# A first stage with VectorE in the program's order, inputs one step ahead, outputs and routing one step later, and joint norms by Newton

## The chip, the cores and the metric

The kernel runs on one core of a Trainium2 chip. The metric is the device time of one execution in microseconds (us), the median of three runs. Engines are named as in the profile: PE is TensorE's matrix products and PEld its weight loads, DVE is VectorE, ACT is ScalarE, POOL is GpSimd, SP is SyncE, which issues most of the DMAs. L404 is line 404 of the kernel before.

## The reference, cut to what matters

Two layers act on x of 8 batches, 512 tokens, 256 channels, in float32. Each layer is an attention and a mixture of experts, both behind a layer norm that is scaled and shifted per batch, and both added back through a gate per batch.

```python
mod = (silu(c) @ wmod).reshape(8, 6, 1, 256)        # sa, ca, ga, sb, cb, gb
h = layernorm(x) * (1 + ca) + sa
x = x + ga * attention(h)
h = layernorm(x) * (1 + cb) + sb
x = x + gb * experts(h)

# layer 0, attention: 16 heads of 64 channels
q = tanh(h @ W_Q) * pi / 4; k = tanh(h @ W_K) * pi / 4      # one number per token and head
heads = cos(q) * cumsum(cos(k) * V) + sin(q) * cumsum(sin(k) * V)
heads /= cos(q) * cumsum(cos(k)) + sin(q) * cumsum(sin(k)) + 1e-6
out = einsum('deh,bthe->btd', W_O, heads)

# layer 0, experts: the best 2 of 4 by softmax; silu(x w1) * (x w3) @ w2
# layer 1, attention: softmax attention in 4 groups of 16 heads, gated
# layer 1, experts: the best 1 of 8 by sigmoid; gelu(x W1) @ W2
```

## The kernel before, in words

The tokens of a batch are four tiles (t) of 128 tokens on the partitions; x of all batches stays in SBUF. A scheduler puts the instructions of each engine into an order. Apart from dependences, that order is its own choice; the program's order (the order in which the Python issues the instructions) is a starting point only. Within an engine's queue, instructions then run in the order chosen.

*The first stage.* Layer 0's attention goes by batch, 0 to 3 (`first`), then most of batch 4, before the first line of experts starts.

- `prepare0(b)` (L329): the norm of b (`norm_T`, with its statistics in `stats`, L175), transposes, the small products `pq`, tanh, then cos and sin by ACT into `tr`, the running sums `pd` by products with a triangle of ones, the denominators `rd` on DVE (L362 to L369), and three sets of rows by token, copied by ACT (L376) and written to DRAM by POOL (L381, L382, `rows`).
- `heads0(b, j)` (L385), eight steps j of two heads each: SP loads `ratio` and `factor`, spread over 64 partitions each, from `rows` (L391); PE makes the values `pv` (L398); DVE runs two scans (L404), which are the two running sums, a multiplication (L407) and an addition (L409) into `hd`.
- `out0(b, t)` (L412): eight products `poa` of `hd` with W_O (L415), then `residual` (L223): DVE multiplies by the gate into `tmp`, of which there are two buffers (L226), and POOL adds it to x (L227).
- `attend0(b)` (L420) runs the eight steps with `prepare0(b + 1)` let in at j = 0, 3 and 5, and then the four `out0`.
- `Moe.route(i)` (L475) for the batch before: norm statistics `stf` of x, the normed rows into `ht`, the slot numbers into `ht` and `ht1` by POOL (L491; `ht1` has one buffer), transposes, the router's product `pl` (L504), softmax and the two best experts by some 24 small DVE instructions (L520 to L558), the ranks `pk` (L563), the positions `pos` (L575) and eight scatters by POOL (L579), which put each token's row at its expert's place in DRAM (`hs`). `table` (L592) makes from the counts the list of expert tiles.
- Beside it: `load_rest`, which holds layer 1's modulation (L136 to L166), and `order_wq`, which reorders a weight.

The loop is `drain(weave(attend0(b), chain(m0.route(b - 1), wq_steps)))`: one step of the side work after each step of the main work. Then route of batch 3, `table`, and seven steps of `a1`, which is `attend0(4)` and what follows.

*The rest.* `Line.run` goes through the list of expert tiles: `xs` loaded by SP (L720), transposed, products `p` (L753), Silu and a multiplication (L758, L760), products `po` (L768), a scaling and a scatter of results. It takes steps of side work (`a1`; later layer 1's attention) between the tiles. Layer 1's attention (`attend`) handles four batches jointly, in two halves; `norm_T` makes their norms. In `stats` ACT takes the square root, DVE the reciprocal, and one Newton step follows:

```python
        nc.scalar.activation(r, v, AF.Sqrt)
        nc.vector.reciprocal(r, r)
        n = wk.tile([P, NT], F32, tag="newton", name=f"newton{nm}")
        nc.vector.scalar_tensor_tensor(n, r, -0.5, r, ALU.mult, ALU.mult)
        nc.vector.tensor_mul(n, n, v)
        nc.vector.scalar_tensor_tensor(r, n, 1.5, r, ALU.add, ALU.mult)
```

Of the kernel before, what the change touches and what calls it, by code (L numbers as in the profile page):

```python
# [9 lines left out]
F32 = mybir.dt.float32  # L10
# [18 lines left out]
def kernel(  # L29
# [99 lines left out]


# [3 lines left out]
    def modulation(l, c, wmod, mp):  # L134
# [4 lines left out]
        for n in range(3):  # L139
# [3 lines left out]
            for kk in range(KD):  # L143
                nc.tensor.matmul(pr[:B, :], sc[:, kk, :], wm[:, kk, :], start=(kk == 0), stop=(kk == KD - 1))
            rows = mp.tile([B, 2, D], F32, tag="rows", name=f"rows{l}_{n}", bufs=1)
            nc.vector.tensor_copy(rows.rearrange("b c d -> b (c d)"), pr[:B, :])
            for i in range(2):
                j = 2 * n + i
                if j % 3 == 1:
                    nc.vector.tensor_scalar(rows[:, i], rows[:, i], 1.0, None, ALU.add)  # L150
                elif j % 3 == 2:
                    sgn = mp.tile([B, D], F32, tag="sgn", name=f"sgn{l}_{j}", bufs=1)
                    nc.vector.tensor_scalar(sgn, rows[:, i], 0.0, 2.0, ALU.is_ge, ALU.mult)
                    mag = mp.tile([B, D], F32, tag="mag", name=f"mag{l}_{j}", bufs=1)
                    nc.scalar.activation(mag, rows[:, i], AF.Abs)
                    nc.vector.tensor_scalar(mag, mag, GATE_MIN, None, ALU.max)
                    nc.vector.scalar_tensor_tensor(rows[:, i], sgn, -1.0, mag, ALU.add, ALU.mult)
            by_channel = [i for i in range(2) if (2 * n + i) % 3 != 2]
            pm = ps_m([P, len(by_channel), KD, B], f"pmT{l}_{n}")
            for m, i in enumerate(by_channel):  # L160
                for k in range(KD):
                    nc.tensor.transpose(pm[:, m, k, :], rows[:, i, k * P : (k + 1) * P], ident[:B, :B])
            at = (0, 2, 3)[n]
            nc.vector.tensor_copy(modT[l][:, at : at + len(by_channel)], pm)
# [10 lines left out]
    def stats(b, nm):  # L175
# [3 lines left out]
        for t in range(NT):  # L179
            nc.vector.bn_stats(st[:, t, :], x[b][:, t, :])  # L180
            nc.vector.bn_aggr(mv[:, t, :], st[:, t, :])
        v = wk.tile([P, NT], F32, tag="var", name=f"var{nm}")
        nc.vector.tensor_scalar(v, mv[:, :, 1], LN_EPS, None, ALU.add)
        r = wk.tile([P, NT], F32, tag="rstd", name=f"rstd{nm}")
        nc.scalar.activation(r, v, AF.Sqrt)
        nc.vector.reciprocal(r, r)
        n = wk.tile([P, NT], F32, tag="newton", name=f"newton{nm}")
        nc.vector.scalar_tensor_tensor(n, r, -0.5, r, ALU.mult, ALU.mult)
        nc.vector.tensor_mul(n, n, v)
        nc.vector.scalar_tensor_tensor(r, n, 1.5, r, ALU.add, ALU.mult)  # L190
        return mv, r

    def normed(b, mv, r, dst, nm):

        sh = wk.tile([P, NT], F32, tag="sh", name=f"sh{nm}")
        nc.vector.scalar_tensor_tensor(sh, mv[:, :, 0], -1.0, r, ALU.mult, ALU.mult)
# [11 lines left out]
    def norm_T(l, b, dst):  # L208


        mv, r = stats(b, f"{l}_{b}")
        xn = wk.tile([P, NT, D], F32, tag="xn", name=f"xn{l}_{b}", bufs=1)
        normed(b, mv, r, xn, f"{l}_{b}")
        for k in range(KD):
            pt = ps_m([P, NT, P], f"pt{l}_{b}_{k}")
            for t in range(NT):
                nc.tensor.transpose(pt[:, t, :], xn[:, t, k * P : (k + 1) * P], ident)
# [5 lines left out]
    def residual(po, gate, b, t, name):  # L223

        tmp = wk.tile([P, D], F32, tag="tmp", name=name, bufs=2)
        nc.vector.tensor_mul(tmp, po, gate)  # L226
        nc.gpsimd.tensor_tensor(x[b][:, t, :], x[b][:, t, :], tmp, ALU.add)  # L227
# [101 lines left out]
    def prepare0(b):  # L329
# [4 lines left out]
        for t in range(NT):  # L334
            for k in range(KD):
                nc.tensor.matmul(
# [21 lines left out]
        nc.tensor.matmul(pd, tri, c, start=True, stop=False)  # L358
        nc.tensor.matmul(pd[:, 1:], ones, before, start=False, stop=True)
        ab = tr[:, :, 2]  # L360
        rd = ap.tile([P, NT, H], F32, tag="rd", name=f"rd{b}", bufs=1)
        nc.vector.tensor_mul(ab, sq, pd)  # L362
        nc.vector.tensor_add(rd, ab[:, :, 0, :], ab[:, :, 1, :])
        nc.vector.tensor_scalar(rd, rd, DEN_EPS * math.sin(2 * ALPHA), None, ALU.add)
        nc.vector.reciprocal(rd, rd)
        nc.vector.reciprocal(tr[:, :, 1], c)
        for i in range(2):
            nc.vector.tensor_mul(ab[:, :, i], sq[:, :, i], rd)
        nc.vector.tensor_mul(ab, ab, c)  # L369
        pt = ps_m([3 * 2 * H, NT, P], f"ptr{b}")  # L370
        for t in range(NT):
            nc.tensor.transpose(pt[:, t, :], tr[:, t].rearrange("p a i h -> p (a i h)"), ident)
# [6 lines left out]
        nc.vector.tensor_mul(rows[1][:, 1:], rows[1][:, 1:], rows[0][:, : S - 1])  # L379
# [5 lines left out]
    def heads0(b, j):  # L385
# [11 lines left out]
        for k in range(KD):  # L397
            nc.tensor.matmul(  # L398
                pv, wv_sb[:, k, j * P : (j + 1) * P], hTs[b][:, k, :],
                start=(k == 0), stop=(k == KD - 1),  # L400
            )
        u = ap.tile([P, 2, S], F32, tag="u", name=f"u{b}_{j}", bufs=2)
        for i in range(2):
            nc.vector.tensor_tensor_scan(  # L404
                out=u[:, i], data0=w[0][:, i], data1=pv, initial=0.0, op0=ALU.mult, op1=ALU.add
            )
        nc.vector.tensor_mul(u, u, w[1])  # L407
        hd = ap.tile([P, S], F32, tag="hd", name=f"hd{b}_{j}", bufs=9)
        nc.vector.tensor_add(hd, u[:, 0], u[:, 1])  # L409
        return hd  # L410

    def out0(b, t, hds, ga):  # L412
        po = ps_o(f"poa{b}_{t}")
        for j in range(NJ):
            nc.tensor.matmul(  # L415
                po, hds[j][:, t * P : (t + 1) * P], wo_sb[:, j, :], start=(j == 0), stop=(j == NJ - 1),
            )
        residual(po, ga, b, t, f"ra{b}_{t}")

    def attend0(b):  # L420

# [3 lines left out]
        for j in range(NJ):  # L425
            hds.append(heads0(b, j))
            if j in (0, 3, 5):
                next(nxt, None)
            yield
        for t in range(NT):  # L430
            out0(b, t, hds, ga)
        yield

    hTs = {}
# [10 lines left out]
    def first_max(v, E, m, o, name):  # L445


        nc.vector.tensor_reduce(m, v, AX.X, ALU.max)
        nc.vector.tensor_tensor(o, v, bcast(m, E), ALU.is_equal)
        nc.vector.tensor_mul(o, o, desc[:, :E].unsqueeze(1).to_broadcast([P, NT, E]))  # L450
        k = wk.tile([P, NT], F32, tag="rm", name=f"k{name}", bufs=4)
        nc.vector.tensor_reduce(k, o, AX.X, ALU.max)
        nc.vector.tensor_tensor(o, o, bcast(k, E), ALU.is_equal)

    class Moe:
# [19 lines left out]
        def route(self, i):  # L475
# [9 lines left out]
            h0 = ht[0]  # L485
            mv, r = stats(b, f"f{bm}")
# [9 lines left out]
            for k in range(KD):  # L496
                pt = ps_m([P, NT, P], f"ptr{bm}_{k}")
                for t in range(NT):
                    nc.tensor.transpose(pt[:, t, :], h0[:, t, k * P : (k + 1) * P], ident)
                by_channel(l, 2, k, b, hT[:, k], pt.rearrange("p t q -> p (t q)"))  # L500
            pl = ps_m([P, NT, E], f"pl{bm}")
            for t in range(NT):
                for k in range(KD):
                    nc.tensor.matmul(  # L504
# [3 lines left out]
            for t in range(0, NT, 2):  # L508
                pb = ps_m([P, 2, D], f"prow{bm}_{t}")
                for q in range(2):  # L510
                    for k in range(KD):
                        nc.tensor.transpose(
# [7 lines left out]
            nc.vector.tensor_tensor(z, pl, b_sb.unsqueeze(1).to_broadcast([P, NT, E]), ALU.add)  # L520
# [6 lines left out]
            if l == 0:  # L527
                s = wk.tile([P, NT], F32, tag="rs", name=f"s{b}")
                nc.vector.tensor_reduce(s, z, AX.X, ALU.max)
                nc.vector.tensor_tensor(z, z, bcast(s, E), ALU.subtract)  # L530
                nc.scalar.activation(z, z, AF.Exp)
                nc.vector.tensor_reduce(s, z, AX.X, ALU.add)
                nc.vector.reciprocal(s, s)
                nc.vector.tensor_mul(z, z, bcast(s, E))
                first_max(z, E, m[0], ch[0], f"a{b}")
                nc.vector.scalar_tensor_tensor(z, ch[0], -2.0, z, ALU.mult, ALU.add)
                first_max(z, E, m[1], ch[1], f"b{b}")
                now = wk.tile([P, NT, E], F32, tag="now", name=f"now{bm}", bufs=2)
                nc.vector.tensor_add(now, ch[0], ch[1])
                nc.vector.tensor_add(s, m[0], m[1])  # L540
                nc.vector.reciprocal(s, s)
                for c in range(C):
                    nc.vector.tensor_mul(ht[c][:, :, D + 1], m[c], s)
            else:
                nc.scalar.activation(z, z, AF.Exp, scale=-1.0)
                nc.vector.tensor_scalar(z, z, 1.0, None, ALU.add)
                nc.vector.reciprocal(z, z)
                first_max(z, E, m[0], ch[0], f"c{b}")
                now = ch[0]
                nc.vector.tensor_copy(ht[0][:, :, D + 1], m[0])  # L550

            pre = fp.tile([P, NT + 1, E], F32, tag=f"pre{E}", name=f"pre{bm}", bufs=3)
            if i == 0:
                nc.vector.memset(pre[:, 0], 0.0)
            else:
                nc.vector.tensor_copy(pre[:, 0], self.run_)
            for t in range(NT):
                nc.vector.tensor_add(pre[:, t + 1], pre[:, t], now[:, t])  # L558
# [3 lines left out]
            nc.tensor.matmul(pk, tri, now, start=True, stop=False)  # L562
            nc.tensor.matmul(pk, ones, pre[:, :NT], start=False, stop=True)  # L563
            yield
            rank = wk.tile([P, NT, E], F32, tag="rank", name=f"rank{bm}", bufs=2)
            nc.vector.tensor_tensor(
# [4 lines left out]
            for c in range(C):  # L571
                nc.vector.tensor_mul(at, ch[c], rank)  # L572
                p_ = fp.tile([P, NT], I32, tag=f"pos{c}", name=f"pos{c}_{bm}", bufs=3)
                with nc.allow_low_precision("whole numbers"):
                    nc.vector.tensor_reduce(p_, at, AX.X, ALU.add)  # L575
# [16 lines left out]
        def table(self):  # L592
# [3 lines left out]
            nc.tensor.matmul(pn, ones, self.run_, start=True, stop=True)  # L596
            n = wk.tile([P, E], F32, tag="cnt", name=f"cnt{nm}", bufs=1)
            nc.vector.tensor_copy(n, pn)
            past_ = fp.tile([1, E1], I32, tag="pasts", name=f"past{nm}", bufs=2)[:, :E]
            nc.vector.scalar_tensor_tensor(past_, n[0:1], 1.0, cbase[0:1, :E], ALU.add, ALU.add)  # L600
            self.past = past_
            cmp_ = wk.tile([P, E, TH], F32, tag="cmp", name=f"cmp{nm}", bufs=1)
            nc.vector.tensor_tensor(
# [3 lines left out]
            nc.vector.tensor_reduce(nt, cmp_, AX.X, ALU.add)  # L607
            upto = wk.tile([P, E, E], F32, tag="upto", name=f"upto{nm}", bufs=1)
            nc.vector.tensor_tensor(
# [3 lines left out]
            nc.vector.tensor_reduce(end, upto, AX.X, ALU.add)  # L613
            base = wk.tile([P, E], F32, tag="base", name=f"base{nm}")
            nc.vector.tensor_sub(base, end, nt)
            full = [P, J, E]

            def of_tile(v, op, rows, dst, name, weigh=None):

                t_ = wk.tile(full, F32, tag="past", name=f"{name}{nm}", bufs=1)  # L620
                nc.vector.tensor_tensor(
                    t_, bcast(rows[:, :J], E), v.unsqueeze(1).to_broadcast(full), op
                )
                if weigh is not None:
                    nc.vector.tensor_tensor(t_, t_, weigh.unsqueeze(1).to_broadcast(full), ALU.mult)
                nc.vector.tensor_reduce(dst, t_, AX.X, ALU.add)
# [4 lines left out]
            nc.vector.tensor_scalar(self.tab[:, 0], which, float(E - 1), None, ALU.min)  # L631
            nc.vector.tensor_scalar(nt, nt, -1.0, float(CAP), ALU.mult, ALU.add)
            skip = wk.tile([P, J], F32, tag="skip", name=f"skip{nm}", bufs=1)
            of_tile(end, ALU.is_ge, iota, skip, "rows", weigh=nt)
            nc.vector.tensor_add(skip, skip, iota[:, :J])
            nc.vector.tensor_scalar(self.tab[:, 1], skip, float(P), float(E * CAP * P), ALU.mult, ALU.min)

            lim = wk.tile([P, E], F32, tag="lim", name=f"lim{nm}", bufs=1)
            nc.vector.scalar_tensor_tensor(lim, base, float(P), n, ALU.mult, ALU.add)
# [3 lines left out]
            nc.vector.tensor_sub(self.used, self.used, skip)  # L643
            self.rest = fp.tile([P, JMAX], F32, tag="rest", name=f"rest{nm}", bufs=2)[:, :J]
            nc.vector.scalar_tensor_tensor(
# [5 lines left out]
        def keep(self, end):  # L651
# [3 lines left out]
            nc.vector.tensor_scalar(  # L655
# [8 lines left out]
            for t, v in zip(k, (self.tab, self.used, self.rest)):  # L664
                nc.vector.tensor_copy(t, v[..., over])
# [602 lines left out]
```

## Time and profile before

| | |
|---|---|
| median of 3 runs | 2013.6 us (2009.74 to 2014.16) |
| the profiled execution | 1998.39 us, span 1996.7 us, mean TensorE clock 0.939 |
| busy, share of the span | PE 88%, PEld 77%, DVE 63%, ACT 37%, POOL 30% |
| first product of the first line of experts (L753) | at 328.9 us of the span |
| first scan (L404) of batch 0; of batch 1 | at 40.7; at 101.9 us |
| first scatter (L579) of batch 3, the last of the first stage | at 307.8 us |
| DMA from issue to landing, 40 to 330 us, medians | `ratio` 5.9, `factor` 4.9, `wm` 6.1, `rows` 4.8, scatters and other users of `hs` 6.7 us |

The profile shows one execution. Its slices are 50 us wide, with the busy share of each engine in tenths; a table by windows gives the same in us. A line of waits reads: engine, tile and line that waited, the engine, tile and line that ended the wait, then total us, times, longest. A line of the timeline reads: start, duration, engine, line, operation, output and inputs, count, and in brackets the idle time before it with what ended it. A releaser is inferred from semaphore events.

### The profile page before, as it was taken

How to read it: one execution, taken by the hardware profiler on the slowest of the kernel's cores; microseconds unless marked ns; L12 is line 12 of the kernel's file. 1: busy time of each engine (PE TensorE's matmuls, PEld its weight loads, DVE VectorE, ACT ScalarE, POOL GpSimd, SP SyncE). 2: the span in 40 equal slices, each digit the busy share in tenths (PEclk: the TensorE clock that was granted, in tenths of full speed). 3: DMA queues.
4: the chain of work that ended last, by engine and by line, in shares of the span. 5: the costliest groups of instructions: out<-in, count | busy, mean ns of one | idle time of the engine just before them, and what ended most of it. 6: DMA issues, size and time to landing. Idle time of an engine off the chain costs nothing. (4 is left out here: it accounts for less than half of the span.)

```text
span 1996.7 us, 32445 instructions
## 1 busy us (share of the span) xinstructions
PE 1757.0 (88%) x11336; PEld 1536.1 (77%) x11336; DVE 1258.1 (63%) x2200; ACT 728.8 (37%) x1384; POOL 594.9 (30%) x564
## 2 busy tenths in 40 slices
PE   6686776999999999989999999997969988898895
PEld 3354435888888889888999889897868877787784
DVE  4786886344433441235999999623499999986200
ACT  5052212231312212226343334622645646454221
POOL 1033132121121121233435444213345464433210
PEclk9797986999999999989999999998989999899898
DMA  7977777899898996896777668799644665579795
GB/s 225 213 206 204 181 185 252 238 315 301 260 307 276 310 332 224 315 323 214 240 246 230 215 229 280 239 320 312 201 132 144 208 202 181 188 241 330 254 348 168
DMA packets 328535, 488.60 MB, mean 245 GB/s; under 512 B 24016, under 2 KB 184048, under 8 KB 327728
## 3 DMA queue, kind: packets, MB, share of 16 engines
q1 hardware_dynamic: 313840, 445.17, 71.6%
q0 software_dynamic: 14528, 41.31, 5.6%
q8 instruction: 92, 1.51, 0.3%
q14 instruction: 75, 0.61, 0.1%
HBM read 446.40 MB, written 45.27 MB: 246 GB/s over the span
## 5 line engine op out<-in xcount | busy, mean ns | idle before, releaser
L753 PE MATMUL p<-xT,w 128*128 128x128 f32 x6144 | 767.5, 281 | 29.7 <-DMA w<-in_W_dram 16.3
L753 PEld LDWEIGHTS p<-xT,w 128*128 128x128 f32 x6144 | 747.0, 198 | 44.4 <-issue 20.1
L768 PE MATMUL po<-w_d,g 128*128 128x256 f32 x1952 | 477.8, 385 | 26.7 <-DVE g L760 16.8
L768 PEld LDWEIGHTS po<-w_d,g 128*128 128x128 f32 x1952 | 355.3, 193 | 78.8 <-DVE g L760 20.5
L783 POOL DMA_INDIRECT ys<-y,to x122 | 153.9, 1261 | 658.3 <-ACT xT L728 420.8
L758 ACT ACTIVATE g<-p 128x512 f32<-128x512 f32 x244 | 145.8, 598 | 462.8 <-PE p L753 432.8
L760 DVE TENSOR_TENSOR g<-g,p 128x512 f32<-128x512 f32 x140 | 95.8, 685 | 274.0 <-PE p L753 253.9
L404 DVE TENSOR_TENSOR_SCAN u<-ratio,pv 128x512 f32<-128x512 f32 x128 | 149.6, 1204 | 57.1 <-PE pv L398 51.4
L989 POOL TENSOR_TENSOR far<-q 128x1024 f32<-128x1024 f32 x64 | 133.1, 2081 | 120.2 <-DVE pr L1047 75.8
L398 PE MATMUL pv<-hT,wv_sb 128*128 128x512 f32 x256 | 138.1, 661 | 33.6 <-DVE u L404 27.5
L415 PE MATMUL poa<-wo_sb,hd 128*128 128x256 f32 x512 | 128.4, 399 | 20.2 <-DVE hd L409 19.7
L775 ACT ACTIVATE y<-po,xs 128x256 f32<-128x256 f32 x122 | 57.8, 473 | 235.8 <-PE po L768 193.2
L579 POOL DMA_INDIRECT hs<-ht,pos x96 | 113.1, 1179 | 93.3 <-DVE at L572 32.4
L415 PEld LDWEIGHTS poa<-wo_sb,hd 128*128 128x128 f32 x512 | 98.3, 198 | 54.2 <-DVE hd L409 33.3
L971 PE MATMUL pqk<-wq_sb,hTa 128*128 128x128 f32 x1024 | 124.8, 281 | 5.1 <-ACT q L978 4.7
L971 PEld LDWEIGHTS pqk<-wq_sb,hTa 128*128 128x128 f32 x1024 | 122.5, 198 | 6.7 <-ACT q L978 5.1
L1024 POOL TENSOR_TENSOR farv<-s,q 128x1024 f32<-128x1024 f32 x32 | 81.7, 2552 | 97.4 <-DVE pr L1021 84.4
L398 PEld LDWEIGHTS pv<-hT,wv_sb 128*128 128x128 f32 x256 | 48.5, 208 | 74.8 <-DVE u L404 35.1
L818 DVE TENSOR_TENSOR yl<-yl,gb 128x512 f32<-128x512 f32 (+1 forms) x24 | 20.6, 866 | 130.8 <-DMA yl<-ys 130.7
L1012 DVE TENSOR_TENSOR s<-s,far 128x1024 f32<-128x1024 f32 x64 | 89.4, 1400 | 0.7 <-POOL far L989 0.7
L758 ACT ACT_TABLE_LOAD x61 | 78.3, 1283 | 6.3 <-PE p L753 5.3
L407 DVE TENSOR_TENSOR u<-u,factor 128x1024 f32<-128x1024 f32 x64 | 78.1, 1220 | 1.4
(203 smaller groups left out, 2013.9 us busy)
## 6 DMA issues: line engine op xcount, KB each, us to landing
w<-in_w_dram SPq DMA_DIRECT2D x280, 512.0 KB, 5.6
w_d<-in_w_dram SPq DMA_DIRECT2D x140, 512.0 KB, 5.8
w<-in_W_dram SPq DMA_DIRECT2D x104, 512.0 KB, 6.0
w_d<-in_W_dram SPq DMA_DIRECT2D x104, 512.0 KB, 6.7
ratio<-rows SPq DMA_DIRECT2D x128, 256.0 KB, 6.7
factor<-rows SPq DMA_DIRECT2D x128, 256.0 KB, 6.4
xs<-hs SPq DMA_DIRECT2D x122, 129.0 KB, 3.4
yl<-ys POOLq DMA_DIRECT2D x32, 256.0 KB, 7.6
```

The costliest lines, as they stand in the source:

```text
L398: nc.tensor.matmul(pv, wv_sb[:, k, j * P : (j + 1) * P], hTs[b][:, k, :], start=(k == 0), stop=(k == KD - 1),)
L404: nc.vector.tensor_tensor_scan(out=u[:, i], data0=w[0][:, i], data1=pv, initial=0.0, op0=ALU.mult, op1=ALU.add)
L415: nc.tensor.matmul(po, hds[j][:, t * P : (t + 1) * P], wo_sb[:, j, :], start=(j == 0), stop=(j == NJ - 1),)
L579: ins = nc.gpsimd.indirect_dma_start(out=self.hs, out_offset=bass.IndirectOffsetOnAxis(ap=pos[c][:, t : t + 1], axis=0), in_=ht[c][:, t, : ...
L753: nc.tensor.matmul(p1[:, f * P : (f + 1) * P], ws[n][:, k, f * P : (f + 1) * P], u["xT"][:, k, :], start=(k == 0), stop=(k == KD - 1),)
L758: nc.scalar.activation(gq, pp[0], AF.Silu if l == 0 else AF.Gelu)
L760: nc.vector.tensor_mul(gq, gq, pp[1])
L768: nc.tensor.matmul(u["po"], u["g"][:, q * NF // 2 + f, :], u["w2"][q][:, f, :], start=(q == 0 and f == 0), stop=(q == 1 and f == NF // 2 - 1),
L783: ins = nc.gpsimd.indirect_dma_start(out=self.ys, out_offset=bass.IndirectOffsetOnAxis(ap=to, axis=0), in_=y, in_offset=None,).ins
L971: nc.tensor.matmul(pq[:, hh], hT[:, k, hb * 4 + hh].rearrange("p b r -> p (b r)"), wq_sb[:, k, i, gh].rearrange("p d w g -> p (d w g)"), s ...
L989: ins = nc.gpsimd.tensor_tensor(t, part(u, 0, d, True), part(u, 1, d, False), ALU.mult).ins
L1012: nc.vector.tensor_add(s, s, far[u, d])
```

## The change

An object `vec` takes VectorE's place in the whole kernel. While `vec.on` holds, from the loop over the first batches until three steps of `a1` behind `table`, every VectorE instruction keeps its place in the program's order. `mat` for TensorE is the same thing and stays off. In that stretch the program itself is written in another order:

- `heads0` is cut in two. `begin0(b, j)` holds the loads of `ratio` and `factor` and the products `pv`; it is called one step before the scans, for the next batch's first step too. `hd` has ten buffers.
- `out0` of a batch is put off to steps 0 and 1 of the next batch, two tiles in each.
- `prepare0` has one break more (behind `pd`) and is let in at j = 0, 2, 3 and 5.
- `route` of layer 0 begins two steps later and has a break behind Exp. It is woven beside `attend0` by itself, and `order_wq` beside both.
- At the end of the stage, steps of `attend0(4)` and of the last `route` alternate by a written list.
- In `stats` with `alone` (the norms of layer 1's second joint half), a first guess is made from the bits of the number, and three Newton steps follow; ACT takes no square root there.

```diff
+            def call(*args, **kw):
+                ins = issue(*args, **kw)
+                if self.on:
+                    tc.keep_in_program_order(ins)
+                return ins
...
+    vec, mat = Ordered(nc.vector), Ordered(nc.tensor)
...
         r = wk.tile([P, NT], F32, tag="rstd", name=f"rstd{nm}")
-        nc.scalar.activation(r, v, AF.Sqrt)
-        nc.vector.reciprocal(r, r)
+        if alone:
+            half = r.bitcast(I32)
+            vec.tensor_scalar(half, v.bitcast(I32), 1, None, ALU.logical_shift_right)
+            with nc.allow_low_precision("a first guess"):
+                vec.tensor_scalar(half, half, -1.0, float(0x5F3759DF), ALU.mult, ALU.add)
+        else:
+            nc.scalar.activation(r, v, AF.Sqrt)
+            vec.reciprocal(r, r)
...
+        for _ in range(3 if alone else 1):
+            vec.scalar_tensor_tensor(n, r, -0.5, r, ALU.mult, ALU.mult)
+            vec.tensor_mul(n, n, v)
+            vec.scalar_tensor_tensor(r, n, 1.5, r, ALU.add, ALU.mult)
...
-    def heads0(b, j):
+    def begin0(b, j):
...
+        begun[b, j] = w, pv
+
+    def heads0(b, j):
+
+        w, pv = begun.pop((b, j))
...
-    def out0(b, t, hds, ga):
-        po = ps_o(f"poa{b}_{t}")
...
+    def out0(b, hds, ga, tiles):
+
+        for t in tiles:
+            po = ps_o(f"poa{b}_{t}")
...
         for j in range(NJ):
+            if (b, j) not in begun:
+                begin0(b, j)
+            if j + 1 < NJ:
+                begin0(b, j + 1)
+            elif b + 1 < B:
+                begin0(b + 1, 0)
             hds.append(heads0(b, j))
-            if j in (0, 3, 5):
+            if j < 2 and pending:
+                out0(*pending[0], range(2 * j, 2 * j + 2))
+                if j:
+                    pending.pop()
+            if j in (0, 2, 3, 5):
                 next(nxt, None)
             yield
-        for t in range(NT):
-            out0(b, t, hds, ga)
-        yield
-
+        pending.append((b, hds, ga))
+        if b + 1 == B:
+            out0(*pending.pop(), range(NT))
+            yield
...
+    vec.on, mat.on = True, False
     for b in first:
-        drain(weave(attend0(b), chain(m0.route(b - 1), wq_steps) if b else rest))
+        drain(weave(weave(attend0(b), m0.route(b - 1)), wq_steps) if b else weave(attend0(b), rest))
...
-    drain(m0.route(HB - 1))
-    m0.table()
...
-    for _ in range(7):
+    last = m0.route(HB - 1)
+    for f in (a1, a1, last, last, last, a1, last, a1):
+        next(f)
+    drain(last)
+    m0.table()
+    for _ in range(3):
         next(a1)
+    vec.on = mat.on = False
```

## The prediction

> **What bounds the kernel now.** The 40 slices of the profile came first: they tell which engine is full where.
>
> ```profile
> PE   6686776999999999989999999997969988898895
> DVE  4786886344433441235999999623499999986200
> ```
>
> A slice is 50 us. From the eighth on TensorE is full; in the first seven (0 to 350 us) no engine is. So this stage is set by order and waits, and what it loses or gains shifts the start of the full part. The table by windows says how full:
>
> ```profile
> 100.00:150.00 50.00, 43.19 (x174) 26.16 (x174) 43.14 (x88) 29.99 (x100) 15.05 (x23) 0.93 0.73 207
> 150.00:200.00 50.00, 34.67 (x134) 23.66 (x134) 31.66 (x90) 13.31 (x24) 16.08 (x23) 0.80 0.75 204
> 250.00:300.00 50.00, 35.10 (x112) 19.14 (x111) 40.23 (x92) 7.33 (x15) 15.80 (x21) 0.83 0.71 183
> ```
>
> Columns: window, us, busy PE, weight load, VectorE, ScalarE, GpSimd, clock, DMA share, GB/s. VectorE is nearest to full, 32 to 43 of 50 us. Its waits, 0 to 350 us:
>
> ```profile
> DVE tr L366 <- ACT tr L348: 19.1, 5, 6.6
> DVE stf L180 <- POOL x L227: 13.9, 11, 4.3
> DVE z L520 <- PE pl L504: 13.4, 4, 7.3
> DVE tr L362 <- PE pd L359: 8.6, 6, 4.0
> ```
>
> (total, times, longest). These 55 us are what an order with inputs a step ahead could win at most. The pace of a head, from VectorE's timeline:
>
> ```profile
> 49.35 2.31 DVE L404 TENSOR_TENSOR_SCAN u<-ratio,pv 128x512 f32<-128x512 f32 x2
> 51.69 1.23 DVE L407 TENSOR_TENSOR u<-u,factor 128x1024 f32<-128x1024 f32 x1
> 52.95 0.69 DVE L409 TENSOR_TENSOR hd<-u 128x512 f32<-128x512 f32 x1
> ```
>
> The next head begins at 53.56, so a head takes 4.22 us. Last, GpSimd's timeline where a batch's rows are scattered:
>
> ```profile
> 252.98 2.00 POOL L579 DMA_INDIRECT hs<-ht,pos  x1 [4.64 <-DVE at L572]
> ...
> 263.62 0.96 POOL L579 DMA_INDIRECT hs<-ht,pos  x1 [0.30 <-issue]
> 271.49 1.04 POOL L491 TENSOR_SCALAR ht<-slot 128x1 f32<-128x1 f32 x4 [6.90 <-DMA hs<-ht,pos]
> 272.61 1.41 POOL L227 TENSOR_TENSOR x<-x,ra 128x256 f32<-128x256 f32 x2
> ```
>
> Eight scatters take 11.6 us; then GpSimd stands 6.9 us until the last has landed, because the slot write of the next batch reuses `ht1`, and the residual adds stand behind it.
>
> **VectorE's work per batch, in program order.** Each term is a count by a row:
> - eight heads, 8 × 4.22 = 33.8;
> - four output gates (L226, 0.43 each) 1.7;
> - two sets of norm statistics: four BN stats at 0.33 (273.36, 273.71 and so on), four aggregates and six small ones at about 0.2 in a dependent chain, 3.3 each, 6.6;
> - `tr` and `rd`, eight instructions, the reciprocal alone 0.95: 2.9; `z` 0.6; `row` 0.6;
> - routing, 24 small ones at 0.2 (300.03 to 304.9): 4.9; positions 1.0.
>
> Sum 52.1 us. The change adds no work here; the waits for ScalarE and TensorE before `tr` and `z` go, since a step of 4.2 us now lies between producer and consumer. (Before, batches 0 to 3 took from 40.73, first scan, to 267.4, the last head's end: 56.7 each, with tail work still owed.)
>
> **The wait it adds.** Outputs of a batch move behind its successor's heads 0 and 1, directly behind the positions of the batch before. In the order of the changed kernel's instructions, GpSimd has the eight scatters, then the slot write, then the adds; VectorE has scan 0, gates of tiles 0 and 1, statistics, scan 1, gates of tiles 2 and 3. `tmp` has two buffers, so the third gate waits for the first add. VectorE is there 4.2 + 0.9 + 3.3 + 4.2 = 12.6 us after the positions. GpSimd: scatters 11.5, landing 6.0 (mean of the four slot-write waits, 23.0 in sum, plus a little work that covered part of one), slot write 1.1, add 0.7: 19.3. Stall 6.7 us, three times (batches 1, 2, 3), and with VectorE in program order nothing passes the waiting gate: scans 2 to 7, `tr`, routing and positions queue behind it, and behind these GpSimd's next scatters. Before, the same landing kept only `stf` waiting (13.9 in all), and scans went past it (274.42).
>
> Here a rule of the Trainium skill speaks against my size. "DMA: Bandwidth & Descriptors", section "Anatomy of one DMA — SWDGE (gpsimd) path", gives about 2.0 us fixed plus bytes over 436 GB/s; 128 rows of 1032 bytes make 0.3, so 2.3 us to landing. By it the stall is 3.0 and three are 9; by the row of 6.9 (mean 6.0) they are 20. The row is of this very DMA with eight in a train: taken. By the rule the end result below would be about 2014, no change.
>
> **Batches in sequence.**
> - Batch 0 as before, to 81.2 (before 82.1).
> - Layer 1's modulation: its VectorE instructions stand in one piece between head 7 and the next scan. Before, `rows` came at 86.91 and the last piece at 107.39, with the scan of 101.89 in between. Its chain (a load of 6.1 us issued once `rows` was read, then a row buffer freed by a 4.8 us write) keeps that pace; I put the next scan at 100.3. Bounds: 90 if loads come early, 107 if the whole chain holds it.
> - Batch 1: 100.3 + 52 = 152. Batches 2 and 3: 58.8 each, 270.
> - Tail: heads 0 to 3 of batch 4, 16.9; gates 1.7; three sets of statistics 9.9; the third stall 6.7; `tr` 2.9; `z`, routing, positions 6.5; waits for Exp and TensorE, no longer covered by scans (Exp 0.2, `pk` 0.5, `pl` 2.6 in the trace): 3; in all 46.7, with 1 for the table's own count, so the scatters begin at about 318, before 307.79: +10.
>
> **SP's queue at the tail.** Before, only half a `ratio` pair stood ahead of the load of the first expert tile, and it did not wait long:
>
> ```profile
> 318.99 0.67 SPq L391 DMA_DIRECT2D ratio<-rows  x1
> 325.30 1.24 SPq L720 DMA_DIRECT2D xs<-hs  x2
> ```
>
> In the changed order `ratio` of batch 5 (it comes a step early, at head 7 of batch 4) stands ahead of `xs`. It waits for `rows` of batch 5, which GpSimd writes behind scatters, landing and slot write: 318 + 10.9 + 6.0 + 1.1, then 1.7 until the row copy (before, 327.45 was 1.7 behind the slot write), 0.6 issue, 4.8 landing = 343. `xs` cannot be issued earlier, though its own rows landed at 335. Before, TensorE's full part began 3.6 behind `xs` (325.30 to 328.89), so it begins at about 346: +17, of which 6.5 is this queue.
>
> **What comes back.** One head more of batch 4 is done before the line (8 steps for 7): two matrix products and four VectorE instructions, about 2 us of TensorE no longer in it (L398 at 0.66 each, and a share of L415). VectorE from 350 to 400 is busy 20 of 50, so nothing there waits for it.
>
> **Norms by Newton.** Four Sqrt switches and the way back to Gelu leave ScalarE:
>
> ```profile
> L185 ACT ACT_TABLE_LOAD  x4: 1283/1283/1283, 1395.7 to 1418.8; - x4
> PE po L768 <- ACT g L758: 4.0, 2, 3.4
> ```
>
> Added: per norm two integer instructions and six for two more rounds, less the reciprocal, seven at 0.2: 1.4, four times, beside a TensorE that is full. The row says what waited: TensorE 4.0 us, twice (waits 1380 to 1480). Bounds: 0, if the stall at 1422 has another cause behind it; 9, if the later attention, VectorE 95% full from 1434 to 1800, hands its start on to the 5.1 us gap of TensorE at 1817. Taken: 4, the stall itself.
>
> **Sum.** +17 − 2 − 4 = +11 us. The profiled execution, 1998.4 us (span 1996.7), becomes about 2010; the median of runs lies 15.2 above that execution, and a difference carries over: 2013.6 + 11.4 = 2025.
>
> **Rivals.** A run of this kernel tells about 0.2%, 4 us, from no change.
> - *As summed*, 2018 to 2034: chance 0.52.
> - *Slower still*, about 2038, 0.16: the modulation chain holds VectorE to 107 (+7), and `tr`, Exp and table switches, no longer passed by scans, cost 2 us a batch more. For it: `z` has waited up to 7.3 and `tr` 6.6. Against: a step lies between.
> - *No change*, 0.10: the landing falls to the 2.3 of the rule, or the queue at SP costs nothing and a stall is half.
> - *Faster*, about 2002, 0.22: VectorE is not held at the third gate. Place: GpSimd's queue behind the scatters. If the first add comes within 12.6 us of the positions, the three stalls (20) are gone, the scatters start at 298, and with the SP queue's 6.5 the gain is 2013.6 + 11.4 − 20 = 2005, 2 to 3 less if a train of scatters that starts in quieter DMA is also faster. It decides from a stall of 3.1 us each: below, the kernel gains. For it: the 55 us of VectorE's waits. Against: 11.5 us of scatter issues alone are nearly the 12.6.
>
> The range takes in faster down to 1998 and slower to 2041.
>
> **What would show it.** VectorE waiting at `ra` for GpSimd's `x` 6 to 7 us, three times, where `stf` waited; waits of `tr` and `z` under 5 us in sum; batches 2 and 3 near 59 us apart; first scatter of the last batch near 318; SP between `ratio` of batch 5 and `xs`; TensorE's first `p` near 346; no Sqrt load at 1395, and the two `po` stalls gone. It is wrong if the gates wait under 3 us, or if `xs` is issued as soon as the scatters land.

## The result and the profile after

The changed kernel takes 2021.28 us, the median of 7 runs (2017.46 to 2026.97); the kernel before takes 2011.57 in the runs beside it. The ratio is 1.0057, 95% interval 1.0041 to 1.0072: slower by 0.57%, where 2025 to 2013.6, also 0.57%, was forecast. The profiled execution took 2017.46 us, span 2015.8, clock 0.937.

Chips differ: beside later runs the kernel before had medians of 2011.1, 2011.2 and, on the last chip, 2001.9. So ratios below are to the kernel before on the same chip. Runs 1, 4, 6 and 9 share one chip, runs 5, 7, 8 and 10 another, runs 2, 3, 11 and 12 a third; for the first traces of the two kernels no chip is on record. Where traces of different chips are set side by side, a few us can be the chip's. In the changed kernel an instruction issued through `vec` or `mat` carries L140, the line of the wrapper; tiles tell them apart.

The slices of the changed kernel, then the window from 300 to 350 us, first of the kernel before, then of the changed one (columns as before):

```profile
PE   6676772999999999989999999998878989799895
DVE  4687887354453431215999999831599999996200
```

```profile
300.00:350.00 50.00, 32.11 (x184) 28.68 (x185) 30.11 (x78) 14.64 (x28) 12.62 (x18) 0.66 0.79 254
300.00:350.00 50.00, 14.02 (x54) 8.53 (x54) 41.73 (x117) 12.34 (x24) 13.31 (x24) 0.60 0.59 156
```

The seventh slice of TensorE fell from 6 to 2: 14.0 us of work where 32.1 stood before. VectorE has 41.7 there for 30.1: the stage ends later, and the experts have not begun beside its last work. VectorE's waits of the first 350 us:

```profile
DVE u L140 <- DMA ratio<-rows: 16.6, 2, 9.0
DVE rows L140 <- PE pmod L140: 14.3, 3, 12.0
DVE ra L140 <- POOL x L253: 7.9, 4, 4.2
DVE tr L140 <- ACT tr L374: 7.6, 1, 7.6
DVE z L140 <- PE pl L140: 6.8, 3, 2.3
DVE s L140 <- ACT z L581: 5.6, 1, 5.6
```

The waits that the new order was to take away went in large part: `tr` for ScalarE from 19.1 to 7.6 (one wait, ahead of the first head), `z` from 13.4 to 6.8 (2.3 in each of three batches), `stf` for GpSimd from 13.9 to nothing. Others came: `rows` for `pmod`, one of the two waits for `ratio` (7.7), the gates `ra`, `s` for Exp. The other wait for `ratio` is no loss:

```profile
40.15 2.33 DVE L140 TENSOR_TENSOR_SCAN u<-ratio,pv 128x512 f32<-128x512 f32 x2 [8.97 <-DMA ratio<-rows]
```

It stands ahead of the first scan, which came at 40.73 in the kernel before, where VectorE waited for other inputs.

In sum the waits hardly grew. From the first scan to the first scatter of batch 3, before and changed:

```profile
40.73:307.79 267.06, 194.26 (x670) 114.95 (x670) 208.59 (x452) 69.75 (x170) 59.89 (x91) 0.83 0.77 196
40.15:327.77 287.62, 199.25 (x726) 120.81 (x726) 224.85 (x487) 96.62 (x210) 58.92 (x98) 0.84 0.71 186
```

VectorE idles 58.5 us of 267.1 before and 62.8 of 287.6 in the changed kernel, but it is busy 208.6 before and 224.9 now: 452 instructions stand there before, 487 now, among them two sets of norm statistics and two of `tr` more. So of the 20.6 us by which this stretch is longer, 16.3 are busy time. The instructions' durations add up to only 8.6 more (231.2 and 239.8); in the kernel before, more of them overlap with their neighbours.

**Where the time went.** One chip ran both kernels once more with a profile (labels before_again and after_again below). Times in us of the span:

| point | before | changed | difference |
|---|---|---|---|
| first scatter of batch 3 | 309.6 | 329.9 | +20.3 |
| first product of the experts | 331.3 | 357.2 | +25.9 |
| 1st result scatter | 350.7 | 376.6 | +25.9 |
| 35th, end of the first line | 869.7 | 888.9 | +19.2 |
| 56th | 1189.7 | 1209.1 | +19.4 |
| 70th, ahead of the joint norms | 1368.7 | 1387.9 | +19.2 |
| 76th, behind them | 1443.1 | 1457.5 | +14.4 |
| 122nd, the last | 1981.2 | 1991.7 | +10.5 |

In this pair the first stage loses 26; the first line gives back 6.7, the stretch with the norms 4.8, the rest 3.9. The first traces of the two kernels give +25.4 at the first product, +25.0 at the 1st result, +24.2 at the 35th, +29.9 and +23.2 around the norms, +19.3 at the last. So the loss of the stage and the gain at the norms repeat; the 6.7 of the first line does not, it is 0.8 there.

### The profile page after: what moved, and what is told of

It reads as the page before. It is cut to its first block, busy times and chain, and to the rows that moved or that the text cites. A ratio compares the mean times of both kernels' runs of the same rounds, so it can differ in the third digit from the quotient of the medians.

```text
span 2015.8 us, 32501 instructions
## 1 busy us (share of the span) xinstructions
PE 1746.8 (87%) x11336; PEld 1528.3 (76%) x11336; DVE 1271.2 (63%) x2228; ACT 727.3 (36%) x1379; POOL 592.8 (29%) x564
## 5 line engine op out<-in xcount | busy, mean ns | idle before, releaser
L140 PE MATMUL p<-xT,w 128*128 128x128 f32 x6144 | 762.8, 281 | 29.5 <-DMA w<-in_W_dram 18.2
L140 PEld LDWEIGHTS p<-xT,w 128*128 128x128 f32 x6144 | 743.4, 197 | 44.5 <-issue 19.9
L140 PE MATMUL po<-w_d,g 128*128 128x256 f32 x1952 | 480.4, 386 | 26.0 <-DVE g L140 17.4
L140 PEld LDWEIGHTS po<-w_d,g 128*128 128x128 f32 x1952 | 354.6, 193 | 77.2 <-DVE g L140 21.5
L140 DVE TENSOR_TENSOR g<-g,p 128x512 f32<-128x512 f32 x140 | 95.4, 682 | 295.6 <-PE p L140 252.8
L140 DVE TENSOR_TENSOR_SCAN u<-ratio,pv 128x512 f32<-128x512 f32 x128 | 149.0, 1205 | 72.5 <-PE pv L140 45.0
L140 PE MATMUL pv<-hT,wv_sb 128*128 128x512 f32 x256 | 140.0, 670 | 32.3 <-DVE u L140 31.7
L630 POOL DMA_INDIRECT hs<-ht,pos x96 | 106.9, 1114 | 115.5 <-DVE at L140 53.1
L140 PE MATMUL poa<-wo_sb,hd 128*128 128x256 f32 x512 | 129.7, 397 | 11.0 <-DVE hd L140 8.9
L826 ACT ACTIVATE y<-po,xs 128x256 f32<-128x256 f32 x122 | 57.7, 473 | 224.7 <-PE po L140 170.5
L140 PEld LDWEIGHTS poa<-wo_sb,hd 128*128 128x128 f32 x512 | 98.3, 199 | 44.5 <-DVE hd L140 16.7
L140 PE MATMUL pqk<-wq_sb,hTa 128*128 128x128 f32 x1024 | 124.4, 281 | 5.1 <-ACT q L1034 4.7
L140 PEld LDWEIGHTS pqk<-wq_sb,hTa 128*128 128x128 f32 x1024 | 121.8, 197 | 6.9 <-ACT q L1034 5.1
L140 DVE TENSOR_TENSOR pr<-s,q 128x1024 f32<-128x1024 f32 x96 | 115.8, 1208 | 0.1
L140 DVE TENSOR_REDUCE o<-pr 128x64 f32<-128x1024 f32 x96 | 115.1, 1207 | 0.0
L140 PEld LDWEIGHTS pv<-hT,wv_sb 128*128 128x128 f32 x256 | 49.4, 210 | 74.9 <-DVE u L140 38.3
L140 DVE TENSOR_TENSOR yl<-yl,gb 128x512 f32<-128x512 f32 (+1 forms) x24 | 20.6, 863 | 130.4 <-DMA yl<-ys 130.3
L140 DVE TENSOR_TENSOR s<-s,far 128x1024 f32<-128x1024 f32 x64 | 89.3, 1398 | 0.7 <-POOL far L1045 0.7
```

Of the source, the lines that this page charges most:

```text
L140: ins = issue(*args, **kw)
L630: ins = nc.gpsimd.indirect_dma_start(out=self.hs, out_offset=bass.IndirectOffsetOnAxis(ap=pos[c][:, t : t + 1], axis=0), in_=ht[c][:, t, : ...
L826: scaled = nc.scalar.mul(y, u["po"], u["xs"][:, D + 1 : D + 2]).ins
```

## The experiments

Ten edits ran, and both kernels once more. Ratios are to the kernel before, with their 95% interval.

**1. The order of VectorE left free.** The edit:

```diff
-    vec.on, mat.on = True, False
+    vec.on, mat.on = False, False
```

> The changed program, but VectorE keeps no order: the scheduler chooses again, as before. Theory 1 (the fixed order of VectorE makes the loss: nothing passes a waiting instruction): the first product of the first expert line, at 353.5 in the changed kernel and 328.9 before, comes at 335 to 342, because the load that waits in SP's queue stays; ratio to before about 1.001. Theory 2 (the rewritten program, with outputs put off and loads ahead, makes it): the product stays near 353 and the ratio near 1.006.

Measured: 1.0053 (1.0032 to 1.0073), the first product at 360.8; run 9, whose first stage is the changed kernel's, has 355.5 on the same chip. VectorE's waits, 0 to 350 us:

```profile
DVE tr L140 <- ACT tr L374: 23.9, 5, 6.6
DVE z L140 <- PE pl L140: 17.9, 4, 7.3
DVE tr L140 <- PE pd L140: 15.7, 5, 9.6
```

Theory 1, which I held, falls: taking the fixed order away does not make this program faster. With the order free, the waits ahead of `tr` and `z` are back and larger than in the kernel before (`stf` is smaller, 6.0 for 13.9), and the loss is the same.

**2. The outputs and routing not put off**, VectorE's order kept. The edit (and the list at the end with two steps of `last` fewer):

```diff
-            if j < 2 and pending:
-                out0(*pending[0], range(2 * j, 2 * j + 2))
...
-        pending.append((b, hds, ga))
-        if b + 1 == B:
-            out0(*pending.pop(), range(NT))
-            yield
+        out0(b, hds, ga, range(NT))
+        yield
...
-            if l == 0:
-                yield
-                yield
```

> The changed kernel with VectorE's order kept, but the outputs of a batch behind its own last head again, and routing at the next batch's first step: the parts that say one step later are undone, inputs still come one step ahead. Theory 1 (postponing is no loss by itself, since VectorE's work is the same and only GpSimd's queue stands in the way): four gates then wait for the products poa, 2 us each in every batch, and the first product comes within 5 us of 354; ratio 1.004 to 1.008. Theory 2 (postponing puts the scatters and all behind them late): scatters of batch 0 start near 150 instead of 161, the first product near 340, ratio 1.000 to 1.003.

Measured: 1.0217 (1.0187 to 1.0246), the first product at 385.8, 28.6 behind the changed kernel on the same chip. Neither theory: it is far worse. Its waits:

```profile
DVE ra L140 <- POOL x L253: 27.4, 6, 9.2
DVE z L140 <- PE pl L140: 16.1, 3, 5.9
...
DVE ra L140 <- PE poa L140: 9.0, 5, 3.5
```

Here two heads and two gates lie between the positions and the third gate: VectorE is there 10.2 us behind the positions, against 12.7 in the changed kernel, where the statistics lie between too. GpSimd still has scatters, landing and slot write ahead of the first add, and the landings take 5.6 to 6.4. The third gate waits 8.5, 8.9 and 9.2. So the wait that the prediction names is real. Against run 12 on the same chip, the gates wait 18.6 longer for GpSimd and 9.0 longer for `poa`, `z` 7.7 longer, and `ratio` 8.3 less: 27 of the 28.6.

**3. The same with the order free.** The edit is that of 2 and of 1 together; the loads a step ahead stay.

> The same, and VectorE's order left to the scheduler: what is left of the change in the first stage is inputs one step ahead, a break more in the preparation, and the list at the end. Theory 1 (inputs ahead lay more on SP's queue and change the scheduler's choice everywhere): the first product at 345 to 360, as with the free order alone (360.8). Theory 2 (the postponed outputs were what made the free order lose): 329 to 338, ratio 0.998 to 1.000.

Measured: 0.9993 (0.9980 to 1.0006), first product at 342.5 (before, same chip: 331.3). Neither theory's product time, but theory 2's ratio. Read together, with Newton in all four:

| | outputs put off | outputs at once |
|---|---|---|
| order fixed | 1.0057 | 1.0217 |
| order free | 1.0053 | 0.9993 |

The two parts act on each other. Under a fixed order putting off gains 1.6%; under a free order it costs 0.6%. The traces suggest why: in the free order no gate waits for GpSimd (that wait is gone from the list), and what is left of putting off is that the scatters of batch 3 begin late (335.4 against 316.4, on two chips). And the kernel before with only Newton (below) has 0.9972, so what is left of the first stage in this run, the loads a step ahead, the added break and the list, seems to cost about 0.2% by itself (two chips, and the intervals just overlap).

**4. The loads of batch 5 not ahead.**

```diff
-            elif b + 1 < B:
+            elif b + 1 < B and b != HB:
```

> The changed kernel, but the first loads of batch 5 are not begun one step ahead, so that no ratio load stands ahead of the expert rows in SP's queue. Theory 1 (the queue holds the expert rows): the first product comes 6.5 earlier, near 347, and the ratio to before falls from 1.0057 to 1.0025. Theory 2 (the expert rows or weights are late anyway): near 353, ratio 1.0057.

Measured: 1.0024 (1.0012 to 1.0035), as theory 1 had it; but the first product comes at 354.4, as theory 2 had it. SP's queue tells why. First the changed kernel, then this one:

```profile
342.85 2.67 SPq L737 DMA_DIRECT2D hs<-hs  x3
348.43 0.65 SPq L418 DMA_DIRECT2D ratio<-rows  x1
349.91 1.25 SPq L771 DMA_DIRECT2D xs<-hs  x2
```

```profile
342.79 1.22 SPq L418 DMA_DIRECT2D factor<-rows  x2
344.53 2.68 SPq L737 DMA_DIRECT2D hs<-hs  x3
350.78 1.22 SPq L771 DMA_DIRECT2D xs<-hs  x2
```

In the changed kernel `ratio` does stand ahead of `xs`, until `rows` have landed. Without it `xs` is not earlier: three copies of blank rows (`tails`, L737) stand behind the `factor` loads of heads 6 and 7, which wait for scans to free their buffers, and `xs` waits for the copies to land. The two hold-ups end within 2 us of each other. So the 0.3% that this edit brings does not come at the first product. Against run 9 on the same chip, this trace is 1.1 us ahead at the first product, 3.5 at the 35th result and 7.0 at the 70th, ahead of the norms. So the gain seems to arise in the lines; what makes it there is not settled, and it is one trace of each.

**5. Neither loads of batch 5 nor heads ahead of the experts.** Edit 4, and the three steps of `a1` behind `table` taken out of the stage (they then run inside the line):

```diff
     m0.table()
-    for _ in range(3):
-        next(a1)
     vec.on = mat.on = False
```

> The changed kernel without the first loads of batch 5 ahead, and without the three steps of batch 4 between the table and the first expert line, so that neither a ratio nor a factor load stands ahead of the copies of blank rows and of the expert rows in SP's queue. Theory 1 (the queue holds the expert rows: first the ratio load, and behind it the copies, which stand behind factor loads that wait for scans): the first product comes at 346 to 348 instead of 354, and the ratio falls 0.1 to 0.2% below 1.0024. Theory 2 (the expert rows are late because the scatters are): 353 and more, and the three steps now lie in the line, ratio 1.003 or above.

Measured: 1.0058 (1.0038 to 1.0078), first product at 349.3, 8.1 earlier than in run 7 on the same chip, whose tail is that of run 4. So SP's queue did hold the expert rows; but the first line, from first to 35th result, takes 529.2 instead of 519.7, and the gain is gone. Three heads more lie in it: TensorE has 12 `pv` products more there (108 for 96), 7.1 us at 0.59 each. The 9.5 us would be 3.2 a head, but that is one pair of traces: a line with no head more took 522.7 in run 6, and in run 10, on this chip, a line with one head more than run 7 took 531.2. So the heads are a likely cause, and their price is not settled.

**6. The slot numbers written later**, so that GpSimd's adds no longer stand behind the landing:

```diff
-            for c in range(C):
+            number(0)
...
+                copied = nc.gpsimd.tensor_copy(ht[1][:, :, :D], h0[:, :, :D]).ins
+                with tc.issue_after(copied):
+                    number(1)
```

> The changed kernel, but GpSimd writes the second set of slot numbers behind the copy of the rows, so that the residual adds no longer stand behind the landing of the scatters. Theory 1 (the gates wait for that landing): VectorE's wait of the third gate, 3.2 and 4.2 us in the second and third place and hidden behind a ratio load in the first, goes; the first product comes about 7 earlier, ratio 1.0022. Theory 2 (VectorE would wait for the next ratio load instead): 0 to 2 us earlier, ratio 1.005.

Measured: the waits of `ra` for GpSimd are gone from the list, the last batch's scatters begin at 324.0 and the first product comes at 350.0, against 329.9 and 355.5 in run 9 on the same chip; the ratio, 1.0051 (1.0032 to 1.0071), does not tell that from nothing. The stall exists and is worth about 5 us of the stage, not 20.

**7. The modulation's loads first.** Edit 4 for batch 0 as well (`b not in (0, HB)`).

> The changed kernel, but the first loads of batches 1 and 5 are not begun a step ahead; so SP issues the loads of layer 1's modulation before those of batch 1. Theory 1 (VectorE's 12 us wait for pmod at 82 comes from these loads standing behind a ratio load that waits for rows): the wait falls to 4 to 6, the scatters of batch 0 start 6 to 8 earlier than 161.3, those of batch 3 near 321, ratio near 1.000 with the 1.0024 of the run without the load ahead at the tail as its point of departure. Theory 2 (batch 1's first scan then waits for its ratio load instead): scatters within 3 of 161.3 and ratio 1.0024.

Measured: 1.0043 (1.0025 to 1.0061), scatters of batch 0 at 162.3. The wait for `pmod` falls as expected:

```profile
DVE u L140 <- DMA ratio<-rows: 20.4, 2, 12.0
...
DVE rows L140 <- PE pmod L140: 9.0, 3, 6.6
...
DVE rows L140 <- DMA md<-rows: 7.2, 1, 7.2
```

but `rows` then waits 7.2 for its write to end, and the next scan comes at 103.7, where run 5 on the same chip has 106.3. Batch 1 then takes 58.6 for 56.6, so the scatters of batch 0 come only 0.7 earlier. That is theory 2's time, but neither its ratio (1.0024) nor its reason: batch 1's first scan does not wait for `ratio`. The `ratio` wait of 12.0, where 7.7 stood, is batch 2's.

**8. All of it mended**: edits 4 to 7, and the fills of result rows (L280) one per batch instead of four behind batch 1.

> The changed kernel with every hold-up taken away together: no loads of batches 1 and 5 a step ahead, the second slot numbers behind the copy of the rows, one fill of the result rows per batch instead of four behind batch 1, and no steps of batch 4 between the table and the first expert line. Theory 1 (the order of VectorE is sound and only what stands ahead of it in other queues makes the loss): scatters of batch 3 at 308 to 314, first product at 327 to 335, ratio 0.997 to 1.000. Theory 2 (waits move to the next input): first product at 340 or later, ratio 1.001 or more.

Measured: 1.0027 (1.0011 to 1.0044), scatters of batch 3 at 317.9, first product at 336.0. The first product lies between the two theories, the ratio is theory 2's. VectorE no longer waits for GpSimd's adds, nor for `ratio` at batch 2. The first product is 21.4 earlier than in run 7, but the first line takes 536.1 us instead of 519.7. Three heads more lie in it, as in run 5, and run 10's line took 531.2 on this chip; how much of the 16.4 is the heads is open. So the hold-ups make most of the stage's loss, and most of what the stage wins is paid back in the line.

How the runs use VectorE between its first scan and the first scatter of batch 3 (us):

| run | length | busy | idle |
|---|---|---|---|
| before (11) | 269.7 | 208.5 | 61.2 |
| changed (12) | 289.6 | 224.7 | 64.8 |
| order free (1) | 295.7 | 212.5 | 83.2 |
| outputs at once (2) | 317.1 | 225.0 | 92.1 |
| outputs at once, order free (3) | 276.2 | 211.0 | 65.1 |
| all mended (8) | 276.6 | 231.0 | 45.6 |

The kernel before has a length of 267.1 in its first trace and 269.1 in run 10, so chips differ little here. With the order free the loss is in waits. With the order fixed VectorE is busy 16 to 23 us longer, and the mended program, which waits 16 us less than the kernel before, is still later. No run takes the two added sets of statistics out of this stretch, so what this would bring is untested.

**9. The square root back in the changed kernel** (`alone=False`).

> The changed kernel with ScalarE's square root back in the joint norms. Theory 1 (Newton gives back 4 us): ratio to before 1.0077 instead of 1.0057, and the waits of po for g near 1420 return, 4.0 in all. Theory 2 (Newton gives nothing, other work fills the gap): ratio 1.0057, no change beyond 0.1%.

Measured: 1.0074 (1.0047 to 1.0102), and TensorE's wait, 1380 to 1480 us, is there again:

```profile
PE po L140 <- ACT g L809: 3.8, 2, 3.4
```

Its interval overlaps the changed kernel's, so the ratio alone does not show Newton's worth; run 10 does.

**10. Newton alone in the kernel before.** The edit is the part of the diff in `stats`, for the second half.

> The kernel before with nothing of the change but the norms by Newton. Theory 1 (Newton gives back what the square roots made TensorE wait, whatever stands ahead of it): 3 to 5 us faster than before, ratio 0.998, and no wait of po for g above 1 us between 1380 and 1480. Theory 2 (the gain in the changed kernel came from its other order): ratio 1.000.

Measured: 2005.72 us against 2011.15, ratio 0.9972 (0.9959 to 0.9984): 5.4 us faster by the medians, and no wait of `po` for `g` is left in that stretch. The stretch from the 70th to the 76th result agrees: it took 74.3 to 76.9 us in the three traces with the square root, 68.8 to 70.0 in the eleven with Newton. This version beats both kernels.

**11 and 12. Both kernels again.**

> The kernel before once more, for a second profile: how much of the first product's time (328.9) and of the first expert line's length (348.4 to 867.6, first to 35th result scatter, 519 us) belongs to one execution. Theory 1: the first stage repeats within 3 us and the line differs by up to 12, as in the kernel with only Newton added (330.9; 531). Theory 2: the line is 519 again, and Newton lengthens it.

> The changed kernel once more, for a second profile: the first product again within 3 us of 354.3, VectorE's waits for pmod (12), ratio (9.0 and 7.7), Exp (5.6) and at the third gate (3.2 and 4.2) again within 1 us each, if they come of the order; otherwise they differ by more.

Measured: before, first product at 331.3 (328.9), first line 519.0 (519.2), TensorE's wait for `g` 4.3; changed, 357.2 (354.3), first line 512.3 (518.5), and VectorE's waits as in the first trace: 12.2 for `pmod`, 8.9 and 8.4 for `ratio`, 6.5 for Exp, 3.7 and 4.7 at the gates. So the stage repeats within 3 us, and its waits come of the order. The line does not repeat as well: the changed kernel's differ by 6.2, and the kernel before with Newton had 531.2 on another chip, though each engine's order of instructions up to the norms is that of the kernel before. A line's length in one trace therefore carries no difference below some 10 us.

## Why the prediction was right, and where its steps were not

The total held: +11.4 forecast, +9.7 by the medians, 0.57% both. That it fits so well is luck, since two errors cancel: the first product came 25 to 26 later where 17 was forecast, and more came back behind it than the 6 forecast. What held is that a loss of the stage shifts the rest. Three programs on one chip lost 11.1, 25.9 and 54.5 us at the first product (runs 3, 12, 2) and 0.8, 10.5 and 41.2 at the last result, so 10 to 15 came back whatever the loss was; in the first pair of traces it was 6.

*Readings and sums.* VectorE is nearest to full in the third of the windows shown; from 150 to 200 us TensorE is busier, 34.7 to 31.7. Of the 19.1 us of `tr` some 12 lie ahead of the first head, where no order of the batches could win them (7.1 from 45 us on). The terms of the tail add up to 47.6 and not 46.7. And the waits before `z` did not go: 2.3 us stayed in each of three batches, 6.8 in sum, where under 5 was forecast for `tr` and `z` together.

*The batches, 52.1 of work.* From scatter to scatter the changed kernel took 63.1, 57.5 and 45.8 for batches 2, 3 and the tail, where 58.8, 58.8 and about 48 stood. In all 166.4 for 166; the sum held better than its reasons. The work itself was sized well: batch 3's 57.5 less its 6.3 of waits is 51.2 for 52.1.

*The wait at the third gate, 6.7 three times.* The mechanism is in the trace: GpSimd's queue, then VectorE's gate.

```profile
291.75 0.96 POOL L630 DMA_INDIRECT hs<-ht,pos  x1 [0.30 <-issue]
297.06 1.03 POOL L541 TENSOR_SCALAR ht<-slot 128x1 f32<-128x1 f32 x4 [4.35 <-DMA hs<-ht,pos]
298.17 2.77 POOL L253 TENSOR_TENSOR x<-x,ra 128x256 f32<-128x256 f32 x4
```

```profile
298.93 0.43 DVE L140 TENSOR_TENSOR ra<-poa,ga 128x256 f32<-128x256 f32 x1 [4.18 <-POOL x L253]
```

The gate begins as soon as the first add is through. But it waits 4.2, at the other place 3.2, and in the first place not at all. VectorE was there 12.7 us behind the positions for 12.6. The mis-sized term is the landing: 7.3, 3.4 and 4.4 us behind the last scatter, where 6.0 was taken; the eight scatters took 10.8 for 11.5. Of the two prices that the prediction weighed, the row's made 6.7, and that of the Trainium skill ("DMA: Bandwidth & Descriptors", section "Anatomy of one DMA — SWDGE (gpsimd) path", an estimate of 2.3 us to landing) made 3.0; the two stalls seen lie between, nearer to the latter, though no landing was as short as 2.3. The landing of 7.3 fell together with another wait:

```profile
157.56 5.27 SPq L280 DMA_DIRECT2D ys<-fill  x3
```

```profile
177.55 2.33 DVE L140 TENSOR_TENSOR_SCAN u<-ratio,pv 128x512 f32<-128x512 f32 x2 [7.66 <-DMA ratio<-rows]
```

Fills of result rows, writes of 1024 KB each, stand ahead of batch 2's loads on SP. The `ratio` load took its 7.7 us of VectorE at the place where I had put the first gate stall. Three fills stood together here; in run 7 four did, and the wait was 12.0; with the fills spread and the queue mended (run 8) it is gone. That it is the fills is argued from this, not tested alone.

*The modulation, next scan at 100.3.* It came at 105.5; the upper bound was 107. The step that failed is "keeps that pace": the first load (`cT`) was issued at 83.8 instead of 75.3. First the kernel before, then the changed one:

```profile
75.27 0.40 SPq L136 DMA_DIRECT2D cT<-in_c_dram  x1
```

```profile
80.73 1.24 SPq L418 DMA_DIRECT2D ratio<-rows  x2
82.48 1.22 SPq L418 DMA_DIRECT2D factor<-rows  x2
83.81 0.53 SPq L155 DMA_DIRECT2D cT<-in_c_dram  x1
```

A `ratio` load of batch 1 stands ahead of it, and waits for `rows` of batch 1, whose multiplication comes at 73.5; the free order had pulled it forward to 48.7. Batch 1 then took 55.8 for 52.

*Exp at the tail.* 3 us were taken for Exp and TensorE together; Exp alone took 5.6.

*The scatters at 318:* 327.8. *The queue at SP, 6.5:* `xs` was issued at 349.9, 7.1 behind the landing (the slot write, which waits for it, begins at 342.8). The prediction's own times make it 8 (335 to 343). The size is near, the holder only half right: taking `ratio` away leaves the copies of blank rows (run 4). The step lacked that the copies now stand behind `factor` loads that wait for scans. *The first product:* 354.3 for 346.

*What comes back, 2 and 4.* One head more would be worth 3.2 by run 5's pair of traces, within what a line varies; the first line gave back 6.7 in one pair of traces and 0.8 in the other. Newton: 4 forecast; 4.8 and 6.7 between the 70th and the 76th result, 0.28% (5.4 us) by run 10. That the norms' stall was the thing to look at held. Another 3.9 come back behind them in both pairs; no run here tells why.

*The rivals.* "Faster" was to be decided at a stall of 3.1 us each; two were 3.2 and 4.2, and without them (run 6) the kernel still lost. So its turning point was misplaced: the stall was not where most of the loss lay. "Slower still" had the modulation and Exp right; their price was in the stage and came back in the line.

## What to carry to other kernels

A fixed order on one engine is only as good as the queues that feed it. Before fixing it, list for every first use of an input what stands ahead of its load on SP and GpSimd, and which wait of another batch that work inherits. Two edits that each look neutral can cancel or multiply: here putting outputs off gained 1.6% under a fixed order and cost 0.6% under a free one, so such parts are tried in all four combinations. A fixed order is judged by the engine's busy time ahead of the point that matters as well as by its waits: here the waits changed places, and work moved ahead of the scatters. And time won ahead of a full engine is checked at the end of the full stretch: in run 8 the first product came 21.4 us earlier than in run 7, and the first line took 16.4 longer.

## What the runs showed of the hardware that was not expected

The landing of a train of eight scatters varied from 3.4 to 7.3 us behind the last issue within one execution. Between chips the same kernel's median differed by 0.5% (2011.1 and 2001.9 us). Taking out four square roots with their switches, 1.28 us each in the trace, gained 5.4 us of the kernel, though ScalarE is busy little more than a third of the span (37%): what counts is that Gelu, for which TensorE waits, stood behind them. In the kernel before, the Gelu at 1421.6 comes behind a switch to the square root at 1418.8 and a switch back at 1420.4. With the same order of instructions on every engine, the first line took 519 us in one execution and 531 in another, on two chips.
